# Linear attention and a Hadamard feed-forward on one core: the running state in split fp32r, and the joints of the feed-forward in another order

## The chip, the cores and the metric

The kernel runs on one core of a Trainium2 chip. The metric is device time in microseconds (us) of one execution, less being better. The core's engines work side by side, each through its own instructions in order: TensorE (PE in the profile, PEld for its weight loads), VectorE (DVE), ScalarE (ACT), GpSimd (POOL). SyncE (SP) issues all DMA transfers of this kernel.

## The reference

One layer of a transformer on 4096 tokens of 512 features: causal linear attention with 16 query heads and 4 key/value heads of 128, then a feed-forward whose inputs pass a Walsh-Hadamard transform; a layer norm follows each. Cut to what matters:

```python
q = rope(x @ Wq.T); k = rope(x @ Wk.T); v = x @ Wv.T      # 16, 4, 4 heads of 128
qf, kf = elu(q) + 1, elu(k) + 1
def step(carry, inp):
    state, z = carry
    q_s, k_s, v_s = inp
    state = state + k_s[..., :, None] * v_s[..., None, :]
    z = z + k_s
    return (state, z), (q_s @ state) / (q_s @ z + 1e-6)
out = scan(step, zeros, (qf, kf, v)) @ Wo.T
x = layernorm(x + out)
h = fwht(x * SU_ug) / 64
h = silu(h @ W_gate.T * sg) * (h @ W_up.T * su)
h = fwht(h * SU_dp) / 64
x = layernorm(x + h @ W_down.T * sd)
```

All is in fp32. The kernel keeps fp32 accuracy on fp32r matmuls by splitting an operand into a high half (rounded to fp32r, an ACT copy) and a low half (the difference, a DVE or POOL subtraction): a product of two such operands takes three matmuls, high x high, high x low and low x high (`hilo` is the helper, lines 95 and 96).

## The kernel before, in words

**Attention** (0 to about 935 us). Two passes `s` over the key/value heads (two of them, `g`, in each pass), each over 16 blocks of 256 tokens: 32 blocks `n`. A block's rows are cut into four chunks of 64 tokens. Within a chunk attention is done by scores: `scores` (lines 380 and 381) multiplies queries with the chunk's keys, `A` is masked by POOL (394). What lies before the chunk comes from the running state, a 128 x 128 matrix per head and chunk: `av` (414) adds q x state and A x v into `ps_num`, and `ps_den` (415) is the denominator.

The state of chunk c is the sum over all tokens before it, plus its first one, so the tiles are shifted by a token: `nat_k` transposes k from its second column on into `kfn`, and `vs` holds v shifted by one row. `state` (337) multiplies `kfn` with `vs` as plain fp32, four matmuls per block and head: rows 0 to 63 and rows 0 to 127 of each half block. DVE adds the state of before (`s32`), ACT and DVE split the result into `sh` and `sl` (353, 355). `vd` holds v's halves for the sums in `av`, each chunk's rows once in the order of the tile; the first row of a chunk is zero there (`rowm_s` is the row mask), since the state holds it already. `proj_v`, `proj_k` and `proj_q` are the projections (241, 288), `rope` rotates.

The main loop runs over 128 slots (n, g, p), two chunks each. A slot issues, in this order: the query projection five slots ahead (`QA`), parts of the next block's k and v and of the states, the scores one slot ahead (`SA`), and `av`. The generators are advanced by hand with `go`; the program is laid out by a scheduler with a simulated timeline, so instructions on one engine may pass each other where an operand is late in that timeline. `pin` keeps an instruction in its written place. In slots 4 to 51 and 62 to 109 `wcomb` sums feed-forward weights on POOL.

**Output projection** (to about 1326 us): 32 tiles of 128 tokens, `wo_tile` (173), `norm_o`, layer norm. Beside it `prep_down` transforms the down weights and `front` (two transposes and a Hadamard matmul per pair of tiles) prepares the feed-forward input for the first three quarters; each quarter is combined for Strassen's scheme with seven products, whose operands are `YKEY`, `WKEY` and the order `SEQ`.

**Up-projection** (to about 1980 us): 32 passes `n` = (quarter f, p), seven products of two matrices (1033). The last four fronts (`ff_front`, i from 12) run inside passes 1 to 6. The results go to `hop_d` in DRAM by `late_puts`, three at a time.

**Down-projection**: eight units (f, jp) of seven products (1187), the first two units interleaved; the operands come back from DRAM (`h_load`, `h_split`, for the first product `h_split_x`), the residual rows by `y_load`, and each product is added to them by `acc` (1197) on DVE. PSUM has eight banks; each stage's pools take them in the order of allocation, so a bank is free once the instruction that last used it in the stage before is done.

Of the kernel before, what the change touches and what calls it, by code (L numbers as in the profile page):

```python
# [20 lines left out]
NB = NTOK // TB  # L21
# [22 lines left out]
def kernel(  # L44
# [3 lines left out]
    cs, ident, had, sel, rowm, out,  # L48
# [30 lines left out]
    rowm_s = cpool.tile([128, 1], F32, name="rowm_s")  # L79
# [8 lines left out]
    def load_raw(src):  # L88
        pool, tag = first.pop(0) if first else (praw, "raw")
        raw = pool.tile([128, 512], F32, tag=tag, name="raw")  # L90
        dma(raw, src)
        return raw
# [86 lines left out]
    with ExitStack() as es:  # L179
# [14 lines left out]
        G.memset(neg1, -1.0)  # L194
        W = {}
# [36 lines left out]
        def proj_v(n):  # L232
# [11 lines left out]
            v32 = pe.tile([128, 2, 256], F32, tag="v32", name="v32")  # L244
            S.activation(v32, ps, AF.Copy)
            vhl = p1.tile([128, 2, 2, 256], F32R, tag="vhl", name="vhl")
            S.activation(vhl[:, 0], ps, AF.Copy, scale=rowm_s)
            yield
            V.scalar_tensor_tensor(vhl[:, 1], ps, rowm_s, vhl[:, 0].bitcast(F32), ALU.mult, ALU.subtract)
            vd = p2.tile([128, 2, 4, 256], F32R, tag="vd", name="vd")  # L250
            for half in range(2):
                for par in range(2):
                    dst = vd[half * 64:half * 64 + 64].rearrange("p l (t r) d -> p l t r d", r=2)[:, :, :, par]
                    dma(dst, vhl[par * 64:par * 64 + 64])
            vs = p1.tile([128, 2, 256], F32, tag="vs", name="vs")
            dma(vs[63:128], v32[0:65])
            dma(vs[0:63, 1], v32[65:128, 0])
            if b:
                dma(vs[0:63, 0], blk[n - 1]["v32"][65:128, 1])
            else:  # L260
                G.memset(vs[0:63, 0], 0.0)
            B.update(v32=v32, vd=vd, vs=vs)

        def rope(ps, csb, f, stay=False):
# [8 lines left out]
            x1 = ps if stay else pe.tile([128, 2, 256], F32, tag="x1", name="x1", bufs=3)  # L273
# [45 lines left out]
        def nat_k(n):  # L319
# [6 lines left out]
            kfn = p1.tile([128, 2, 2, 128], F32, tag="kfn", name="kfn")  # L326
            S.activation(kfn, pt, AF.Copy)
            B["kfn"] = kfn
            B["S"] = []

        def state(n, g):
# [3 lines left out]
            for i in range(4):  # L335
                r = slice(0, 64 * (i % 2) + 64)
                T.matmul(ps[:, i], B["kfn"][r, g, i // 2], B["vs"][r, i // 2, g * 128:(g + 1) * 128],  # L337
                         start=True, stop=True)
# [16 lines left out]
            V.tensor_tensor(sl, s32, sh.bitcast(F32), ALU.subtract)  # L355
# [41 lines left out]
        def av(n, g, p):  # L397
# [19 lines left out]
            num = p3.tile([128, 4, 2, 64], F32, tag="num", name="num")  # L417
# [3 lines left out]
            if p == 1:  # L421
                ds = pout.tile([4, 256], F32, tag="ds", name="ds", bufs=2)
# [53 lines left out]
        first.extend([(praw, "raw")] * 3 + [(p3, t) for t in ("num", "s32", "sh", "sl") for _ in range(3)])  # L476
# [7 lines left out]
        dma(rowm_s, rowm)  # L484
# [27 lines left out]
        run(proj_v(0))  # L512
        weights_q(0, 0)
# [4 lines left out]
        nat_k(0)  # L518
# [15 lines left out]
        for i, (n, g, p) in enumerate(slots):  # L534
# [18 lines left out]
            if sl == (0, 0):  # L553
# [6 lines left out]
                gs2 = state(n, 1)  # L560
                go(gs2)
# [7 lines left out]
            elif sl == (1, 0):  # L569
                if nxt:  # L570
                    nat_k(n + 1)
            else:
                gs1 = state(n + 1, 0) if nxt else None
                go(gs1)
# [11 lines left out]
            elif sl == (0, 1):  # L586
                go(gv)
            elif sl == (1, 1):
                go(gs1)
            av(n, g, p)  # L590
# [112 lines left out]
    def front(i, y2, spool, ptr, phd, alloc):  # L703
        f, c = divmod(i, 4)
        d = alloc[1]([128, 2, 4, 128], F32, "fd")
        for e in range(2):
# [7 lines left out]
            yield  # L714
            ps = phd([128, 4, 128], "ps_hd")
# [68 lines left out]
    with ExitStack() as es:  # L784
        p2 = late["c2"] = es.enter_context(tc.tile_pool(name="c2", bufs=2, reuse_waits="tile"))
        pwo = es.enter_context(tc.tile_pool(name="pwo", bufs=3, space=PSUM, reuse_waits="tile"))
        pfd = es.enter_context(tc.tile_pool(name="pfd", bufs=1, space=PSUM, reuse_waits="tile"))
        pon = es.enter_context(tc.tile_pool(name="pon", bufs=2, space=PSUM, reuse_waits="tile"))

# [184 lines left out]

    def h_split_x(n, his, los):
        HOP[n, 0] = []
        for qd, raw in enumerate(HR.pop((n, 0))):
            hi, lo = (x[qd // 2][:, 2 * (qd % 2):2 * (qd % 2) + 2] for x in (his, los))
# [3 lines left out]
    with ExitStack() as es:  # L982
# [8 lines left out]
        def ff_front(i):  # L991
            y2 = []
            for e in range(2):
                y = utile("y_nat")
# [11 lines left out]
        for n in range(NS):  # L1006
# [11 lines left out]
            if n in (1, 2, 4, 5):  # L1018
                step(fr, 9)
                fr = ff_front(12 + (1, 2, 4, 5).index(n))  # L1020
            new = {}
            for s, tag in enumerate(SEQ):
# [41 lines left out]
                if p == 7:  # L1064
# [4 lines left out]
                    elif s == 0:  # L1069
                        hx = [xtile([128, 4, 256], F32R, "hxh") for _ in range(2)]  # L1070
                        hx += [ytile([128, 4, 256], F32R, x) for x in ("hxl", "hxl", "hxh", "hxh", "hxl", "hxl")]
                        h_split_x(0, hx[0:2], hx[2:4])
                        h_load(1, 0)
                    elif s == 2:
                        split_b(0)
                        load_b(1)
                    elif s == 3:
                        h_split_x(1, hx[4:6], hx[6:8])
# [25 lines left out]
    with ExitStack() as es:  # L1104
# [6 lines left out]
        def y_load(n):  # L1111
            f, jp = units[n]
            YN[n] = []
            for half in range(2):
                y = (pd.tile([128, 2, 512], F32, tag="yn", name="yres") if half else
                     xtile([128, 2, 512], F32, "yres"))
                for j in range(2):
                    dma(y[:, j], y_d[8 * f + 2 * (2 * jp + j) + half])
                YN[n].append(y)

# [7 lines left out]
        def finish(n, half):  # L1128
            f, jp = units[n]
            y = YN[n][half]  # L1130
# [21 lines left out]
        y_load(0)  # L1152
        y_load(1)
        for idx, (n, s) in enumerate(order):
# [8 lines left out]
            if idx > 0:  # L1163
                for put in late_puts[:3]:
                    put()
# [103 lines left out]
```

## Time and profile before

| | before |
|---|---|
| median of 3 runs | 2309.88 us (2309.2 to 2312.54) |
| the profiled execution | 2307.71 us |
| its span in the profile | 2306.0 us |
| granted TensorE clock, mean | 0.994 |
| PE, DVE, ACT, POOL busy | 2260.5, 1765.5, 1394.5, 1281.7 us |
| DMA queue | 481.45 MB, 68.0% of 16 engines |

A row of the profile names a line of the kernel, the engine, the operation, the tiles (result<-operands), the shape and the count; then its busy time, the mean of one in ns, and the time for which the engine was idle before such instructions, with what ended it. Matmuls are pipelined, so their durations overlap: two that start 0.11 us apart can show 0.28 us each. In the chain of waits each instruction has the time from the one before it.

### The profile page before, as it was taken

To read this page: it belongs to the slowest core of one execution; us is meant where nothing else is said; L and a number is where in the kernel's file an instruction comes from. 1 tells how busy PE (TensorE), PEld (TensorE's weight loads), DVE (VectorE), ACT (ScalarE), POOL (GpSimd) and SP (SyncE) were. 2 spreads that over 40 slices of the span, in tenths; PEclk is the share of its full clock that TensorE was granted. 3 is DMA by queue.
4 is the path that set the end of the run, shared out by engine and by line. 5 is a ranking of instruction groups with operands and counts; after the bars stand their busy time and mean duration, and the time that the engine had idled before them with its cause. 6 is when DMAs were issued, how large, how long until landed. Compare 5 with 4: busy or idle time off the path is not lost.

```text
span 2306.0 us, 42216 instructions
## 1 busy us (share of the span) xinstructions
PE 2260.5 (98%) x14432; PEld 2005.5 (87%) x14432; DVE 1765.5 (77%) x2684; ACT 1394.5 (60%) x2515; POOL 1281.7 (56%) x1063
## 2 busy tenths in 40 slices
PE   8999999999999999899999999999999999899998
PEld 7999999899999998688878878788788888899998
DVE  8888888888888878688898766776766766675555
ACT  7777777777777767344443566655555655464553
POOL 5556666555555546468787435665555555633332
PEclk9999999999999999999999999999999999999999
DMA  6665665555655554889988976876766757887673
GB/s 195 176 180 171 181 185 173 165 157 150 168 168 150 161 152 130 309 268 270 291 282 262 294 240 212 249 244 192 227 209 187 224 186 212 265 274 242 227 253 119
DMA packets 369527, 484.15 MB, mean 210 GB/s; under 512 B 68670, under 2 KB 224384, under 8 KB 365344
## 3 DMA queue, kind: packets, MB, share of 16 engines
q1 hardware_dynamic: 369312, 481.45, 68.0%
q8 instruction: 114, 1.87, 0.3%
q14 instruction: 101, 0.83, 0.1%
HBM read 282.76 MB, written 156.76 MB: 191 GB/s over the span
## 4 chain that ended last, share of the span: by engine, by line
PE 88%; DMA 5%; DVE 3%; POOL 2%; ACT 1%; issue 1%; SPq 0%; POOLq 0%; DVEq 0%; ACTq 0%
PE ps_qk L288 17%; PE ps_a L1033 14%; PE ps_wo L173 13%; PE ps_da L1187 7%; PE ps_b L1033 7%; PE ps_num L414 6%; PE ps_v L241 4%; PE ps_s L337 4%; PE ps_c L1033 4%; PE ps_db L1187 4%; PE ps_dc L1187 2%; PE ps_sc L380 1%; PE ps_sc L381 1%; PE ps_den L415 1%; DMA rb<-rec_d 1%
## 5 line engine op out<-in xcount | busy, mean ns | idle before, releaser
L288 PE MATMUL ps_qk<-xh,wh 128*128 128x256 f32 x1280 | 355.6, 278 | 0.0
L288 PE MATMUL ps_qk<-xl,wh 128*128 128x256 f32 x1280 | 355.3, 278 | 0.0
L288 PE MATMUL ps_qk<-xh,wl 128*128 128x256 f32 x1280 | 354.7, 277 | 0.0
L394 POOL TENSOR_SCALAR_AFFINE_SELECT A<-A 64x512 fp32r<-64x512 f32 x256 | 212.1, 829 | 241.0 <-DVE am L390 144.2
L96 DVE TENSOR_TENSOR wol<-A,woh 128x512 fp32r<-128x512 f32 x217 | 229.0, 1060 | 108.8 <-ACT woh L95 95.5
L1015 POOL TENSOR_TENSOR cc<-cc 128x512 f32<-128x512 f32 x96 | 149.9, 1562 | 285.8 <-ACT cc L1012 162.4
L270 POOL TENSOR_TENSOR sw<-sw,csb 128x512 f32<-128x512 f32 x160 | 208.0, 1300 | 135.3 <-ACT sw L269 121.3
L288 PEld LDWEIGHTS ps_qk<-xh,wh 128*128 128x128 f32 x1280 | 241.0, 188 | 3.1
L288 PEld LDWEIGHTS ps_qk<-xh,wl 128*128 128x128 f32 x1280 | 240.8, 188 | 0.9
L288 PEld LDWEIGHTS ps_qk<-xl,wh 128*128 128x128 f32 x1280 | 240.9, 188 | 0.3
L95 ACT ACTIVATE woh<-A 128x512 fp32r<-128x512 f32 x217 | 135.6, 630 | 131.3 <-PE ps_b L1033 76.7
L95 ACT ACTIVATE hah<-hraw 128x512 fp32r<-128x512 f32 x216 | 133.2, 629 | 120.1 <-PE ps_da L1187 55.5
L96 POOL TENSOR_TENSOR hal<-hraw,hah 128x512 fp32r<-128x512 f32 x78 | 105.8, 1360 | 179.3 <-PE ps_da L1187 64.1
L1033 PE MATMUL ps_a<-yoh,woh 128*128 128x512 f32 x512 | 202.2, 396 | 2.6 <-DVE yp L901 2.3
L1033 PE MATMUL ps_a<-yol,woh 128*128 128x512 f32 x512 | 202.5, 395 | 0.0
L1033 PE MATMUL ps_a<-yoh,wol 128*128 128x512 f32 x512 | 199.6, 395 | 0.0
L96 DVE TENSOR_TENSOR hal<-hraw,hah 128x512 fp32r<-128x512 f32 x138 | 110.5, 811 | 90.9 <-PE ps_da L1187 34.0
L173 PE MATMUL ps_wo<-wh,oh 128*128 128x512 f32 x372 | 148.5, 399 | 3.1 <-ACT oh L95 3.1
L1040 ACT ACTIVATE sv<-ps_a,wsc 128x512 f32<-128x512 f32 x192 | 127.2, 680 | 39.3 <-PE ps_a L1033 39.2
L173 PE MATMUL ps_wo<-wh,ol 128*128 128x512 f32 x372 | 147.8, 397 | 0.0
L173 PE MATMUL ps_wo<-wl,oh 128*128 128x512 f32 x372 | 147.8, 397 | 0.0
L271 DVE TENSOR_TENSOR ps_qk<-ps_qk,csb 128x512 f32<-128x512 f32 x160 | 111.2, 695 | 33.0 <-ACT sw L269 31.9
(280 smaller groups left out, 7359.5 us busy)
## 6 DMA issues: line engine op xcount, KB each, us to landing
hraw<-hop_d SPq DMA_DIRECT2D x224, 256.0 KB
vd<-vhl SPq DMA_DIRECT2D x128, 256.0 KB
num_d<-num SPq DMA_DIRECT2D x128, 256.0 KB
rb<-rec_d SPq DMA_DIRECT2D x128, 256.0 KB
hop_d<-hS SPq DMA_DIRECT2D x128, 256.0 KB
nt<-num_d SPq DMA_DIRECT2D x31, 1024.0 KB
A<-in_wug_dram SPq DMA_DIRECT2D x93, 256.0 KB
hop_d<-cc SPq DMA_DIRECT2D x64, 256.0 KB
```

The lines of the kernel that those rows point to most:

```text
L95: i = S.activation(hi, src, AF.Copy)
L96: j = eng.tensor_tensor(lo, src, hi.bitcast(F32), ALU.subtract)
L173: T.matmul(ps, l[:, h], r, start=i == 0, stop=i == 47)
L270: G.tensor_tensor(sw, sw, sinb, ALU.mult)
L271: V.tensor_tensor(ps, ps, cosb, ALU.mult)
L288: T.matmul(ps[:, j], W[key][wa][:, k * 128:(k + 1) * 128], B[xa][:, k], start=i == 0, stop=i == 11)
L394: G.affine_select(ah, ah.bitcast(F32), pattern=[[0, 8], [1, 64]], compare_op=ALU.is_ge, fill=0.0, base=0, channel_multiplier=-1)
L414: T.matmul(ps[:, c2], l, r, start=i == 0, stop=i == len(ops) - 1)
L1015: G.tensor_tensor(x, x, c.pop(("g", q)), ALU.mult)
L1033: T.matmul(ps, w[:, u, k], y[:, k], start=first and i == 0, stop=i == 5, skip_group_check=not first)
L1040: S.activation(x, ps, AF.Copy, scale=sc)
L1187: T.matmul(ps[:, j], ops[qd][al][:, r, js], BW[s][bl][ip], start=first and i == 0, stop=i >= 45 or last and i == 23, skip_group_check=True)
```

## The change

Five things are changed.

1. The running state is made from split halves. `kfn` holds a high and a low half of k, `vst` a high and a low half of shifted v, each twice (index `u`): once with rows 64 to 127 zero (for the boundary in the middle of a half block), once whole. So both states of a half block come from one matmul of 256 columns, three of them for the three products. The fp32 copy `v32` and the tile `vs` are gone.
2. `vst`, `vcar` and the two tiles `VD` last for the whole stage; their zero rows are written once at the start by DVE and ACT, so the row mask `rowm` is gone, and the transfers leave those rows out. `vcar` carries the tail of v from block to block.
3. The low half of every second state (`sl`, g = 1) is subtracted by POOL in place of DVE. The low half of k is a new subtraction on DVE.
4. Buffers: `num` has two in place of three, `ds` one for two, `x1` two for three.
5. Joints: the PSUM pool `pwo` is allocated after `pfd` and `pon`; the last four fronts start in passes 1, 3, 5, 8 in place of 1, 2, 4, 5, take their rows into raw buffers, and wait one step more before their Hadamard matmul; the first h halves go to raw and weight buffers; `y_load` is made for half a unit at a time, for the first two units within the last up pass; the sum of product (2, 0) is put off by one product; the last block's second state is made a slot earlier.

```diff
@@ setup of attention
+        vst = pe.tile([128, 2, 2, 2, 256], F32R, name="vst", bufs=1)
+        vcar = pe.tile([128, 2, 256], F32R, name="vcar", bufs=1)
+        VD = [p2.tile([128, 2, 4, 256], F32R, tag="vd", name="vd") for _ in range(2)]
+        def zero(eng, dst):
+            src = ones4[0:dst.shape[0], 0:1, None].to_broadcast(list(dst.shape))
+            if eng is S:
+                S.activation(dst, src, AF.Copy, scale=0.0)
+            else:
+                V.tensor_scalar(dst, src, 0.0, None, ALU.mult)
+        for l in range(2):
+            for k in range(2):
+                zero(S if k else V, VD[k][:, l])
+                zero(S if k else V, vst[64:128, l, k, 0:1])
+            zero(S, vst[0:64, l, 0])
@@ proj_v
-            v32 = pe.tile([128, 2, 256], F32, tag="v32", name="v32")
-            S.activation(v32, ps, AF.Copy)
-            S.activation(vhl[:, 0], ps, AF.Copy, scale=rowm_s)
+            S.activation(vhl[:, 0], ps, AF.Copy)
             yield
-            V.scalar_tensor_tensor(vhl[:, 1], ps, rowm_s, vhl[:, 0].bitcast(F32), ALU.mult, ALU.subtract)
+            V.tensor_tensor(vhl[:, 1], ps, vhl[:, 0].bitcast(F32), ALU.subtract)
+            vd = VD[n % 2]
             for half in range(2):
                 for par in range(2):
-                    dma(dst, vhl[par * 64:par * 64 + 64])
+                    dst = vd[half * 64 + 1:half * 64 + 64].rearrange("p l (t r) d -> p l t r d", r=2)[:, :, :, par]
+                    dma(dst, vhl[par * 64 + 1:par * 64 + 64])
-            dma(vs[63:128], v32[0:65])
-            dma(vs[0:63, 1], v32[65:128, 0])
-            if b:
-                dma(vs[0:63, 0], blk[n - 1]["v32"][65:128, 1])
+            dma(vst[63:128, :, :, 1], vhl[0:65])
+            dma(vst[63:64, :, :, 0], vhl[0:1])
+            for u in range(2):
+                dma(vst[0:63, :, 1, u], vhl[65:128, :, 0])
+                if b:
+                    dma(vst[0:63, :, 0, u], vcar[0:63])
...
+        def carry(n):
+            if n < N and n % NB < NB - 1:
+                dma(vcar[0:63], blk[n]["vhl"][65:128, :, 1])
@@ nat_k
-            S.activation(kfn, pt, AF.Copy)
+            kfn = pe.tile([128, 2, 2, 2, 128], F32R, tag="kfn", name="kfn", bufs=1)
+            S.activation(kfn[:, 0], pt, AF.Copy)
...
+            yield
+            V.tensor_tensor(kfn[:, 1], pt, kfn[:, 0].bitcast(F32), ALU.subtract)
@@ state
-            for i in range(4):
-                r = slice(0, 64 * (i % 2) + 64)
-                T.matmul(ps[:, i], B["kfn"][r, g, i // 2], B["vs"][r, i // 2, g * 128:(g + 1) * 128],
-                         start=True, stop=True)
+            for j in range(2):
+                for i, (k, v) in enumerate(((0, 0), (0, 1), (1, 0))):
+                    T.matmul(ps[:, 2 * j:2 * j + 2], B["kfn"][:, k, g, j], vst[:, v, j, :, g * 128:(g + 1) * 128],
+                             start=i == 0, stop=i == 2)
...
-            V.tensor_tensor(sl, s32, sh.bitcast(F32), ALU.subtract)
+            (G if g else V).tensor_tensor(sl, s32, sh.bitcast(F32), ALU.subtract)
@@ main loop: nat_k is a generator, its second part a few instructions later
             elif sl == (1, 0):
                 if nxt:
-                    nat_k(n + 1)
+                    gn = nat_k(n + 1)
+                    go(gn)
+                    carry(n + 1)
@@ front
             hilo(hl[:, 0], hl[:, 1], ps)
             yield
+            if i >= 12:
+                yield
@@ output projection
-        pwo = es.enter_context(tc.tile_pool(name="pwo", bufs=3, space=PSUM, reuse_waits="tile"))
...

+        pwo = es.enter_context(tc.tile_pool(name="pwo", bufs=3, space=PSUM, reuse_waits="tile"))
@@ up-projection
-            if n in (1, 2, 4, 5):
-                step(fr, 9)
-                fr = ff_front(12 + (1, 2, 4, 5).index(n))
+            if n in (1, 3, 5, 8):
+                step(fr, 12)
+                fr = ff_front(12 + (1, 3, 5, 8).index(n))
...
                     elif s == 0:
-                        hx = [xtile([128, 4, 256], F32R, "hxh") for _ in range(2)]
+                        hx = [praw.tile([128, 2, 256], F32R, tag="raw", name="hxh") for _ in range(3)]
+                        hx.append(wres.tile([128, 2, 256], F32R, tag="w", name="hxh"))
...
                         h_load(1, 0)
+                        y_load(0, 0)
+                        y_load(1, 0)
@@ down-projection
-        y_load(0)
-        y_load(1)
...
+            if s == 1 and n < 2:
+                y_load(n, 1, pd)
...
+            if todo:
+                acc(*todo)
+                todo = None
+            if s == 0 and n == 2:
+                todo = (y0, lo, ps)
```

## The prediction

> **What bounds the kernel now.** I read the engine totals first, then the table by stretches of time, then the chain of waits inside one block of attention, then PE's gaps one by one. Engine totals (busy us, share of the span, instructions):
>
> ```profile
> PE 2260.5 (98%) x14432; PEld 2005.5 (87%) x14432; DVE 1765.5 (77%) x2684; ACT 1394.5 (60%) x2515; POOL 1281.7 (56%) x1063
> ```
>
> PE is idle for 45.5 us in all, so whatever removes PE time is worth its full length as long as no other engine becomes the bound. The stretches (length, then busy us of PE, PEld, DVE, ACT, POOL, clock, DMA share, GB/s) show where another engine is near:
>
> ```profile
> 130.00:230.00 100.00, 100.00 (x819) 95.20 (x819) 89.50 (x141) 74.77 (x140) 59.60 (x58) 1.00 0.57 164
> 530.00:630.00 100.00, 100.00 (x816) 94.79 (x814) 85.99 (x137) 71.88 (x133) 53.36 (x57) 1.00 0.56 155
> 930.00:1030.00 100.00, 92.76 (x408) 73.37 (x407) 74.42 (x120) 43.67 (x87) 55.21 (x41) 0.98 0.88 295
> 1930.00:2030.00 100.00, 93.58 (x614) 85.77 (x613) 63.89 (x70) 51.71 (x91) 61.84 (x43) 0.97 0.82 250
> ```
>
> In attention (0 to 930 us) PE is full, but DVE stands at 86 to 90%. The two other rows are the joints between stages, where PE loses 7.2 and 6.4 us. The chain of waits in attention (start, length, what) lies wholly on PE; one stretch of it:
>
> ```profile
> 569.77 2.72 PE ps_qk L288 x24
> 572.50 1.67 PE ps_s L337 x8
> 574.16 0.36 PE ps_num L414 x3
> ```
>
> and the rows of the running state and of a projection, by form:
>
> ```profile
> L288 PE MATMUL ps_qk<-xh,wh 128*128 128x256 f32 x1280 | 355.6, 278 | 0.0
> L337 PE MATMUL ps_s<-vs,kfn 128*128 128x128 f32 x256 | 62.3, 325 | 0.0
> L337 PE MATMUL ps_s<-vs,kfn 64*128 64x128 f32 x256 | 62.1, 322 | 1.1 <-ACT kfn L327 0.6 <-DVE s L348 0.5
> ```
>
> The means overlap, since matmuls are pipelined; prices come from the chain. A state has four fp32 matmuls of 128 columns, recorded as eight (512 records for 32 blocks x 2 groups x 4), and takes 1.67 us: 0.209 us a record. The 24 projection matmuls (fp32r, 256 columns) take 2.72 us: 0.113 each.
>
> **The change part by part.**
>
> *Running state on PE.* A block of 256 tokens takes 28.02 us on the chain (projection of v to projection of v, 560.97 to 588.99). Two states take 3.34 of it; its other 212 records share 24.68 us, 0.116 each. After, a state is six fp32r matmuls of 256 columns (three products for each of two token halves): 6 x 0.116 = 0.70 us. Saved: 2 x (1.67 - 0.70) = 1.94 us a block, over 32 blocks 62.2 us. The Trainium skill speaks against this: "FP8 and Floating Point Precision", section "TensorE Precision Notes", counts a true fp32 matmul as four passes; with the 55.6 ns between 128-column matmuls that "TensorE: Matmul & The Clock Gate" gives (section "Wait — 56ns, not 53.3ns?"), a state is an estimated 4 x 4 x 0.056 = 0.89 us and the whole change would be worth only 64 x (0.89 - 0.70) = 12 us. The trace has 1.67 us for the same thing, and the row decides: 62 us.
>
> *DVE.* Added per block: the low half of k, a subtraction read from PSUM; nearest row `ql<-ps_qk`, 685 ns, so 32 x 0.685 = +21.9 us. The low half of v loses its row mask: 746 to about 685 ns, -2.0. Half of the `sl` subtractions go to POOL: 32 x 0.891 = -28.5. Sum -8.6 us. *POOL* gains 32 subtractions with two SBUF inputs; its own rows for that shape run 1.36 us (`hal`) to 1.68 (`xl`); at 1.45 it is +46 us, from 56 to about 66% of a shorter stage. What that does to DVE I can only bound: DVE's `ql<-sw,qh` (two SBUF inputs) averages 979 ns, `ql<-ps_qk,qh` 685. The skill ("SBUF — State Buffer", "Who interferes with whom") says that a DVE instruction with two SBUF inputs contends with a POOL instruction that reads SBUF and that the loser blocks fully: as a worst case the whole 46 us would come back on DVE. By the row, about 0.3 us is lost per such instruction with POOL 60% busy; 8 points more POOL give some 0.04 us on six instructions, 0.2 us a block, +6 us. I take the row. DVE's total in attention thus stays at about 803 - 9 + 6 = 800 us, while PE's need falls to 930 - 62 = 868: 92%. In the first half of attention, where x is also split, it is worse: the block at 203 to 231 us shows 25.19 us of DVE, which becomes about 25.1 of 26.1, 96%.
>
> *ACT* loses the fp32 copy of v (597 ns x 32 = 19 us) and the masked scale (682 to 597 ns, 3 us): 72% before, no limit.
>
> *SP and the copies of v.* Before: three `vs` transfers and four `vd` a block. After: `vd` stays at four; `vst` takes one of 65 rows, one of a single row, two of 63 rows, two more from the carry tile where a block precedes, and the carry tile itself one: seven in place of three. SP's rows price an issue:
>
> ```profile
> 564.68 1.63 SPq L58 DMA_DIRECT2D vs<-v  x2
> 566.40 3.40 SPq L58 DMA_DIRECT2D vd<-vhl  x4
> ```
>
> 0.82 to 0.85 us each, so 7 x 0.84 - 2.47 = +3.4 us a block. Adding up SP's rows for the block 561 to 589 gives 18 us; it becomes 21.6 of 26.1. Behind those seven stand the stores of `num` and `ds`, the x loads two blocks ahead, the wcomb loads and stores. `num` (three buffers to two), `ds` (two to one) and `x1` (three to two) are reused 13, 13 and some 13 us later, and ACT waited only 1.9 us in all for a `num` store: priced at nothing while SP's lag stays below a slot of 6.5 us; at most 1 us a block, 30 us, if it does not. The bytes added, about 0.65 MB a block, raise a DMA share of 0.57 by some 0.08: cover enough. One-tile `vhl` and `kfn` were one-tile before.
>
> *Friction in attention.* With DVE at 92 to 96% and SP at 83%, PE will not stay gapless. Bounds: 3 us (as gapless as now) and 58 us (DVE keeps all the idle time it has now, see the rival). In the densest stretch that the trace has, DVE is 90% busy and PE shows no gap, so I am nearer the low end: 0.7 us a block in the first half, 0.25 in the second, +15 us.
>
> *Start.* Zeroing the lasting tiles costs ACT about 4 us and DVE 3; ACT is free from 2.1 to 3.4 us, DVE to 4.1 us, so +1.5 (0 to 3).
>
> *Joints*, from PE's gaps in the timeline (start, length, what, gap before it and its releaser), and DVE's row that explains the largest:
>
> ```profile
> 1328.49 0.50 PE L1033 MATMUL ps_a<-yoh,woh 128*128 128x512 f32 x1 [2.26 <-DVE yp L901]
> 1376.21 0.50 PE L716 MATMUL ps_hd<-fhl,hadr 128*128 128x512 f32 x1 [1.34 <-ACT fhl L95]
> 1383.51 0.66 PE L709 MATMUL ps_tr<-idt,y_nat 128*128 128x128 f32 x4 [0.95 <-DMA y_nat<-y_d]
> 1986.43 0.58 PE L1187 MATMUL ps_dc<-wdh,hal 128*128 128x256 f32 x1 [5.21 <-DVE hal L96]
> 2072.86 0.38 PE L1187 MATMUL ps_da<-wdh,hah 128*128 128x256 f32 x1 [1.16 <-DVE yres L1197]
> 1984.19 0.69 DVE L1197 TENSOR_TENSOR yres<-ps_da,yres 128x512 f32<-128x512 f32 x1 [5.14 <-DMA yres<-y_d]
> ```
>
> The PSUM pools of the output projection swap places, so that the first feed-forward banks were last used by `pfd`, not by the last `ps_wo`: 2.26 us. The fronts inside the up-projection get one more step before their Hadamard matmul and start further apart, with y in the raw buffers: 1.34 + 0.95. At the start of the down-projection DVE stood behind a sum whose `yres` rows were asked for only at 1978.9 us; the loads for both first units move to the last up-projection pass, ahead of the h loads: up to 5.21, and the smaller wait of 1.21 before it. The deferred sum of (2, 0) takes away 1.16. Together 12.1 us. The loads moved go past the `hop_d` stores and h loads on SP, so what is late next may be an h tile (POOL waited up to 4.5 us for `hraw`), and the h halves of the two first units now sit in raw and weight buffers, which must be free: I count 9, with 3 and 13 as ends. The 3.10 us at 945.83 (output projection behind `rec_d` loads) is not touched in its cause; nothing.
>
> **Sum.** -62.2 + 15 + 1.5 - 9 = -54.7 us against the profiled execution (2307.71 us; span 2306.0). That gives 2253.0; the median of the runs, 2309.88, lies 2.2 above that execution, so 2255 us. About 0.2% (5 us) is what a measurement of this kernel can tell from no change.
>
> **The rivals.**
> *DVE becomes the bound.* If DVE keeps the idle time that it has (2.8 us of the 28 at 203 to 231, 4.2 at 561 to 589, most of it short waits for ACT's `sw` and `qh`), a block takes 25.1 + 2.8 = 27.9 in the first half and 23.7 + 4.2 = 27.9 in the second, and attention gains 0.1 x 32 = 4 us; halfway between this and gapless is a gain of 33. Against the extreme: those waits are for results of PE work, which now comes sooner. With half: -33 + 1.5 - 9 = -40, 2269; the extreme is 2298. Chance of a result nearer to this than to the forecast: 0.2.
>
> *The copies of v land too late (slower).* After the change the state needs `vst`, which is filled from the split v, behind four `vd` issues on the same queue. v's low half is ready near 565.7 in the block shown; eight issues at 0.84 us end at 572.4. The chain's DMA pieces run from issue to use 4.1 us (`raw<-in_x_t`) to 4.9 (`rb<-rec_d`), so the last copy lands at about 576.9, while PE comes to the state at 572.5: 4.4 us of stall in 31 blocks, +136 against -70 of the other terms, 2375 us. It decides from 2.2 us of stall a block. Against it: the state is first read at 583.5 (`ps_num<-qh,sh` after the next group's scores), so 8 us of slack lie behind it, and the order of instructions is laid out by a simulated timeline that already slips projections between scores and sums where an operand is late; if it puts the state a few matmuls later, nothing waits. Chance 0.1, with 2315 to 2375 as its range.
>
> *The six new matmuls are not cheaper.* If a state matmul keeps 0.209 us whatever its type, six take 1.25 us and the gain is 64 x 0.42 = 27 us; less 8 of friction: -27 + 8 + 1.5 - 9 = -26, 2283. Against it: every fp32r row of 256 columns runs at 0.113 to 0.127. Chance 0.04.
>
> **How the numbers follow.** Forecast 0.66 (2238 to 2268), DVE bound 0.2 (2262 to 2298), price kept 0.04, late copies 0.1. Faster: 0.66 + 0.2 + 0.04 less a little for the extreme ends, 0.88; slower 0.1; same 0.02. The range takes in friction at 3 and joints at 13 with the start at nothing (2309.9 - 62.2 + 3 - 13 = 2238) and, above, most of the DVE case: 2238 to 2288. What is left out is the late copies and the DVE extreme, under 2 in 10.
>
> **What the changed profile would show.** Right: `ps_s` as 384 records of 128x256, 0.70 us for six on the chain; blocks 26 to 27 us apart; DVE at 91 to 95% in attention, POOL at 65%; no gap above 2 us near the start of the down-projection. DVE bound: PE below 97% busy in the first half, its gaps released by DVE (`A`, `sl`, `ql`). Late copies: gaps before `ps_s` released by DMA `vst`. Wrong altogether: a span above 2300 with PE gapless, that is, new PE time that I do not see in the diff.

## The result, and the profile after

| | before | after |
|---|---|---|
| median of the runs | 2309.54 us (2308.2 to 2312.54) | 2439.75 us (2438.14 to 2441.04) |
| ratio, with 95% interval | 1 | 1.0561 (1.0545 to 1.0577) |
| span of the profiled execution | 2306.0 us | 2439.3 us |
| granted TensorE clock, mean | 0.994 | 0.961 |
| first matmul of the output projection (`ps_wo`) | 945.8 us | 1085.3 us |

The changed kernel is 130 us slower, where 55 us less was forecast. All of it lies in attention: the first `ps_wo` comes 139.5 us later, and what follows is 6.1 us shorter than before. It is the rival of the late copies, which had a chance of 0.1, and it is 65 us dearer than priced there.

The page of the kernel after: engine totals, the granted clock in 40 slices (tenths of full speed), and the group of the running state:

```profile
PE 2279.3 (93%) x14304; PEld 2054.8 (84%) x14304; DVE 1750.5 (72%) x2690; ACT 1380.9 (57%) x2489; POOL 1310.5 (54%) x1093
...
PEclk9989999999999989899999999999999999999999
...
L358 PE MATMUL ps_s<-vst,kfn 128*128 128x256 f32 x384 | 79.4, 337 | 117.4 <-DMA vst<-vhl 106.6
```

PE is idle for 160 us where it was for 45.5, and its busy time has not gone down by the 62 us that the cheaper state should save: it went up by 19. The second number says that something else slowed the matmuls. Busy time hides that, so the stretches by clock come next (columns as before: length, then busy us of PE, PEld, DVE, ACT, POOL, clock, DMA share, GB/s), at the times shown of before (at 930 us the kernel after is still in attention):

```profile
130.00:230.00 100.00, 89.73 (x691) 87.67 (x691) 76.55 (x120) 63.77 (x119) 55.71 (x54) 0.91 0.55 171
530.00:630.00 100.00, 87.56 (x677) 85.63 (x676) 70.54 (x117) 59.65 (x109) 46.41 (x49) 0.91 0.48 147
930.00:1030.00 100.00, 87.76 (x685) 86.18 (x685) 73.59 (x120) 60.54 (x113) 48.53 (x51) 0.91 0.49 145
1930.00:2030.00 100.00, 100.00 (x430) 80.53 (x429) 69.98 (x78) 57.30 (x93) 54.81 (x36) 1.00 0.69 215
```

In attention two things are wrong at once: PE is idle for 10 to 12% of the time, and the granted clock is 0.91 on the mean where it was 1.00. DVE, ACT, POOL and the DMA engines are all less busy than before, so none of them is the bound. The waits of PE (total us, times, longest) name what it waits for:

```profile
PE ps_s L358 <- DMA vst<-vhl: 106.6, 39, 4.8
PE ps_w L172 <- ACT qh L94: 7.3, 1, 7.3
PE ps_v L256 <- ACT wh L94: 7.2, 1, 7.2
PE ps_dc L1226 <- DVE hal L95: 5.4, 1, 5.4
```

One block shows how the wait comes about. First SP's queue in the timeline (start, length, what):

```profile
614.68 4.20 SPq L58 DMA_DIRECT2D vd<-vhl  x4
618.98 3.73 SPq L58 DMA_DIRECT2D vst<-vhl  x4
622.82 1.74 SPq L58 DMA_DIRECT2D den_d<-ds  x2
```

then PE's timeline in the same block:

```profile
621.73 0.28 PE L307 MATMUL ps_qk<-xh,wh 128*128 128x256 f32 x1
626.17 0.98 PE L358 MATMUL ps_s<-vst,kfn 128*128 128x256 f32 x3 [4.16 <-DMA vst<-vhl]
626.94 0.41 PE L307 MATMUL ps_qk<-xl,wh 128*128 128x256 f32 x1
627.16 0.41 PE L307 MATMUL ps_qk<-xh,wl 128*128 128x256 f32 x1
...
629.81 0.28 PE L435 MATMUL ps_num<-qh,sh 128*128 128x256 f32 x1
629.92 0.28 PE L435 MATMUL ps_num<-ql,sh 128*128 128x256 f32 x1
```

v's low half is ready at 614.66. SP issues the four `vd` transfers first, at 1.05 us each, then the four `vst` transfers, until 622.71; the state starts 3.46 us after that. PE reached it at 622.01 and stood for 4.16 us. The rows behind show the second cost: matmuls of 256 columns start 0.22 us apart at 626.94, and 0.12 us apart again from 629.2 on. The records of the clock show it as well. The wait fills the stretch of the first row here, and in the next 3.41 us the granted clock is 0.50 (columns as above):

```profile
622.26:625.67 3.41, 0.00 (x0) 0.00 (x0) 1.22 (x2) 0.41 (x1) 1.80 (x2) 1.00 0.59 146
625.67:629.09 3.42, 2.92 (x14) 2.95 (x15) 0.00 (x0) 0.00 (x0) 0.00 (x0) 0.50 0.78 238
629.09:632.50 3.41, 3.41 (x30) 3.34 (x30) 3.02 (x6) 2.50 (x5) 0.94 (x2) 1.00 0.90 245
```

The old kernel had written the same order (`vd`, then the shifted copies), but its copies read `v32`, the fp32 copy that ACT finished 1.6 us before the split halves, and the scheduler had pulled them ahead; that is why its SP rows show `vs` before `vd`. The change made both sets of transfers read `vhl`. They now become ready together, and the written order stands.

What does the new state cost where nothing is late? This one, 20 us earlier in the trace after, is not held up:

```profile
602.51 0.88 PE L358 MATMUL ps_s<-vst,kfn 128*128 128x256 f32 x6
603.23 0.28 PE L401 MATMUL ps_sc<-qh,khl 128*128 128x256 f32 x1
```

0.72 us for six matmuls, against 1.67 before. The saving that the change was priced at is there.

### The profile page after: what moved, and what is told of

It is laid out like the page before. It is cut to its first block, busy times and chain, and to the rows that moved or that the text cites. A ratio compares the mean times of both kernels' runs of the same rounds, so it can differ in the third digit from the quotient of the medians.

```text
span 2439.3 us, 42199 instructions
## 1 busy us (share of the span) xinstructions
PE 2279.3 (93%) x14304; PEld 2054.8 (84%) x14304; DVE 1750.5 (72%) x2690; ACT 1380.9 (57%) x2489; POOL 1310.5 (54%) x1093
## 5 line engine op out<-in xcount | busy, mean ns | idle before, releaser
L307 PE MATMUL ps_qk<-xh,wh 128*128 128x256 f32 x1280 | 374.1, 292 | 0.0
L307 PE MATMUL ps_qk<-xh,wl 128*128 128x256 f32 x1280 | 373.6, 292 | 0.0
L307 PE MATMUL ps_qk<-xl,wh 128*128 128x256 f32 x1280 | 373.4, 292 | 0.0
L415 POOL TENSOR_SCALAR_AFFINE_SELECT A<-A 64x512 fp32r<-64x512 f32 x256 | 199.1, 778 | 250.6 <-DVE am L411 194.1
L307 PEld LDWEIGHTS ps_qk<-xh,wh 128*128 128x128 f32 x1280 | 256.1, 200 | 2.7
L307 PEld LDWEIGHTS ps_qk<-xl,wh 128*128 128x128 f32 x1280 | 256.8, 201 | 1.0
L307 PEld LDWEIGHTS ps_qk<-xh,wl 128*128 128x128 f32 x1280 | 256.1, 200 | 0.8
L358 PE MATMUL ps_s<-vst,kfn 128*128 128x256 f32 x384 | 79.4, 337 | 117.4 <-DMA vst<-vhl 106.6
L358 PEld LDWEIGHTS ps_s<-vst,kfn 128*128 128x128 f32 x384 | 64.4, 231 | 126.0 <-issue 98.7
L369 DVE TENSOR_TENSOR s<-ps_s,s 128x256 f32<-128x256 f32 x124 | 51.7, 417 | 140.1 <-PE ps_s L358 139.5
```

Of the source, the lines that this page charges most:

```text
L307: T.matmul(ps[:, j], W[key][wa][:, k * 128:(k + 1) * 128], B[xa][:, k], start=i == 0, stop=i == 11)
L358: T.matmul(ps[:, 2 * j:2 * j + 2], B["kfn"][:, k, g, j], vst[:, v, j, :, g * 128:(g + 1) * 128], start=i == 0, stop=i == 2)
L369: V.tensor_tensor(s32[:, i:i + 2], ps[:, i:i + 2], prev.to_broadcast([128, 2, 128]), ALU.add)
L415: G.affine_select(ah, ah.bitcast(F32), pattern=[[0, 8], [1, 64]], compare_op=ALU.is_ge, fill=0.0, base=0, channel_multiplier=-1)
```

## The experiments

Theory after the first look: the place of `vst` in SP's queue makes PE wait, and the half clock after each wait makes it dearer. Rivals: the number of transfers (seven or more for three) or the load on DVE makes the kernel slow whatever the order; or the clock falls for another reason and the waits follow from it.

**e1: the `vst` transfers ahead of the `vd` transfers.** The only edit is that the lines of `vst` stand above the `vd` loop in `proj_v`.

```diff
+            dma(vst[63:128, :, :, 1], vhl[0:65])
+            dma(vst[63:64, :, :, 0], vhl[0:1])
...
             for half in range(2):
                 for par in range(2):
                     dma(dst, vhl[par * 64 + 1:par * 64 + 64])
-            dma(vst[63:128, :, :, 1], vhl[0:65])
-            dma(vst[63:64, :, :, 0], vhl[0:1])
...
```

Expected:

> The changed kernel with one edit: in proj_v the vst transfers are issued ahead of the four vd transfers. Theory A (the state waits because its copies stand behind vd on the SP queue, 4 x 1.05 us, and the idle stretch lets the TensorE clock drop): the wait for vst shrinks from 4.1 us a block to under 1, the clock returns to 0.99, 2240 to 2275 us. Theory B (the copies land late by themselves, small rows and a long way from issue to landing, wherever they stand): a gap of 2 to 3 us a block stays, over 2330 us. Theory C (DVE or SP is the bound once the state is cheap): no wait for vst, but PE gaps released by DVE, 2275 to 2310 us.

Measured: 2322.8 us, ratio 1.0049 (1.0033 to 1.0064), clock 0.983. No wait for `vst` is left, and 117 us are back. But it is still slower than before. The waits of ACT in e1 name a new one:

```profile
ACT num L439 <- DMA num_d<-num: 64.8, 19, 6.3
```

and an instance of it, SP first, then ACT, both from the timeline:

```profile
596.75 3.33 SPq L58 DMA_DIRECT2D vst<-vhl  x4
600.13 4.97 SPq L58 DMA_DIRECT2D vd<-vhl  x4
605.20 0.66 SPq L58 DMA_DIRECT2D num_d<-num  x1
```

```profile
611.42 0.60 ACT L439 ACTIVATE num<-ps_num 128x512 f32<-128x512 f32 x1 [4.42 <-DMA num_d<-num]
```

Eight transfers in a row hold SP for 8.4 us, the store of `num` stands behind them, and with two `num` buffers in place of three ACT stops for 4.42 us; `sh` and `A` are then late for PE, which waits 8.3 us for `sh` and 17.5 us for `A` in e1. Whether a third `num` buffer alone would have taken ACT's wait away was not tried. So e1 separates the two parts of SP's trouble: `vst` behind `vd` stops PE at once, and eight transfers in one burst stop ACT.

**e9: the old kernel with its copies kept behind `vd`.** The opposite of e1, made on the kernel before: fp32 state, three `vs` transfers, old joints. The last argument of `dma` keeps a transfer in its written place.

```diff
-                    dma(dst, vhl[par * 64:par * 64 + 64])
+                    dma(dst, vhl[par * 64:par * 64 + 64], True)
-            dma(vs[63:128], v32[0:65])
-            dma(vs[0:63, 1], v32[65:128, 0])
+            dma(vs[63:128], v32[0:65], True)
+            dma(vs[0:63, 1], v32[65:128, 0], True)
```

Expected:

> The kernel before (fp32 state, three vs and four vd transfers, old joints) with one thing changed: the two vs transfers of a block are kept behind its four vd transfers on SP's queue. In the kernel before they stand ahead, because the fp32 copy of v is ready 1.6 us before the split halves. Theory (the place in the queue is what costs, not the number of transfers and not the new matmuls): in the block at 561 to 589 us of before, vd would be issued from 566.4 to 569.8, vs to 571.4, and land 3.5 us later (the time that the kernel after shows from the last vst issue to the state's start), at 574.9; the state stands at 572.5, or some 0.7 us later where projections pass it: 1.7 to 2.4 us of wait for DMA vs a block, 50 to 75 us in all, and some matmuls at half clock on top. 2360 to 2400. Rival (the seven transfers or the DVE load made the kernel after slow): no wait above 0.5 us a block, 2310 to 2320.

Measured: 2371.55 us, ratio 1.0246 (1.0203 to 1.0290), clock 0.980. The state's group by form, and one block of PE's timeline:

```profile
L337 PE MATMUL ps_s<-vs,kfn 64*128 64x128 f32 x256 | 65.1, 336 | 41.4 <-DMA vs<-v 20.2 <-ACT qh L366 11.3 <-issue 5.3
```

```profile
583.38 2.07 PE L337 MATMUL ps_s<-vs,kfn 64*128 64x128 f32 x8 [1.58 <-DMA vs<-v]
585.10 0.56 PE L288 MATMUL ps_qk<-xl,wh 128*128 128x256 f32 x1
585.46 0.41 PE L380 MATMUL ps_sc<-qh,khl 128*128 128x256 f32 x1
585.67 0.41 PE L381 MATMUL ps_sc<-ql,khl 128*64 128x256 f32 x1
```

The order alone costs the old kernel 63 us. Counted from the starts of PE's records, the waits before the first matmul of a state add up to 46 us (1.4 in before), 1.5 a block and a little under the 1.7 to 2.4 expected. Matmuls at half clock add some 24 us (how this is counted stands in the section on the prediction). The rival that blamed the number of transfers or DVE falls: neither was changed here. The state does not read `qh`, which the row also names; a wait for several semaphores is put down to one of them, and how much of those 11.3 us is the copy of v is not told by the row.

**e2: the state made later.** The state of head group 0 is moved from the block before to the first slot of its own block, some 34 matmuls later on PE; SP's order stays as in the kernel after.

```diff
-                gs1 = state(n + 1, 0) if nxt else None
-                go(gs1)
+                gs1 = None
...
+                if n:
+                    gs1 = state(n, 0)
+                    go(gs1)
+                    go(gs1)
+                    go(gs1)
```

Expected:

> The changed kernel with the transfers as they are, but the state of head group 0 moved from the last slot of the block before into the first slot of its own block: some 34 matmuls (about 4 us) later on PE, still ahead of its first reader. Theory A: a wait of 4.1 us is covered by 4 us of other matmuls, 2245 to 2290 us. Theory B gives the same here if its lateness is the same 4 us; a queue that falls further behind with every block (SP saturated) would give 2350 us or more. If the early place of the state is needed (its readers wait for sh and sl instead), PE gaps of about 3 us before ps_num, over 2350 us.

Measured: 2375.22 us, ratio 1.0282 (1.0259 to 1.0306), clock 0.975. From PE's waits:

```profile
PE ps_s L358 <- DMA vst<-vhl: 55.0, 39, 3.5
```

The wait is halved, not gone: as many times, half as long. This is what the prediction's argument of slack amounts to when it is tried: moving the state back by some 34 matmuls, 4 us at 0.12 each, takes half of the wait away. The rest is lost because the copies come later too: in the block at 577 to 593 us v's low half is ready 4.8 us after the projection of v on PE, where the block shown of the kernel after has 2.7. Why DVE makes it later was not traced.

**e3: other work in front of the state.** 32 matmuls whose result is overwritten by the state, put ahead of the state of head group 0 in each block; they add work and change nothing in what the kernel computes (`FILL` is 32).

```diff
+            if g == 0 and n:
+                for i in range(FILL):
+                    T.matmul(ps[:, 0:2], W["q", s, 0, i % 4][0][:, 0:128], B["xh"][:, i % 4], start=True, stop=True)
```

Expected:

> The changed kernel with 32 extra fp32r matmuls of 256 columns per block ahead of the state of head group 0, written to its PSUM bank and overwritten by it: 3.7 us of PE work that should lie inside the wait. It measures the clock by itself. If the drop of the granted clock after each idle stretch is a cost of its own (about 160 us more at half clock than before, so some 75 us of work lost): 2350 to 2385 us, mean clock 0.98 or more. If the waits alone are the cost: 2430 to 2450 us, with the idle time turned into busy time.

Measured: 2488.39 us, ratio 1.0766 (1.0746 to 1.0786), clock 0.974. PE's wait for `vst` fell to 56.9 us, but in 55 places where it was 39. The layout moved the state as well: these matmuls begin 76 behind v's projection in nearly every block, where the state of the kernel after stands 78 to 98 behind it. It was to show the clock by itself and does not: waits and clock went down together. Inconclusive.

**e5: `vst` first, and `vd` a slot later.** e1's order, and the `vd` transfers taken out of `proj_v` and issued for the next block after the low half of its k.

```diff
+        def put_vd(n):
+            vd, vhl = blk[n]["vd"], blk[n]["vhl"]
+            for half in range(2):
+                for par in range(2):
...
+                    dma(dst, vhl[par * 64 + 1:par * 64 + 64])
...
                     go(gn)
                     carry(n + 1)
+                    put_vd(n + 1)
```

Expected:

> e1 (vst first) with the four vd transfers not behind vst at once, but after the low half of k, a slot later; they are first read a slot and more after that. In e1 no wait for vst is left, but ACT waited 64.8 us in all for num_d stores before it could write num (two buffers) again, because those stores stood behind vst and vd on the SP queue; DVE, PE and the clock then followed. Theory D (the queue of SP, through num, is what is left of the loss): ACT's wait for num_d falls to under 20 us, 2240 to 2285 us. Theory C (DVE is the bound): no change beyond 10 us, 2310 to 2325.

Measured: 2274.65 us, ratio 0.9849 (0.9831 to 0.9866), clock 0.991: 165 us less than the kernel after, 35 less than before. A stretch of attention in e5:

```profile
530.00:630.00 100.00, 100.00 (x851) 99.00 (x850) 91.19 (x147) 74.92 (x137) 59.34 (x62) 1.00 0.65 194
```

PE is gapless at full clock with all the transfers of the change still there and DVE at 91%. In its timeline SP issues the two sets apart, with the `num` and `den` stores between them:

```profile
580.97 3.38 SPq L58 DMA_DIRECT2D vst<-vhl  x4
584.45 0.44 SPq L58 DMA_DIRECT2D num_d<-num  x1
584.99 0.58 SPq L58 DMA_DIRECT2D den_d<-ds  x2
585.62 0.81 SPq L58 DMA_DIRECT2D vcar<-vhl  x1
586.48 4.38 SPq L58 DMA_DIRECT2D vd<-vhl  x4
```

Same bytes, same count, another order: this settles the main cause.

**e6: `vd` spread over two later slots.** As e5, but two of the four transfers at the end of each of the block's last two slots.

```diff
+            if g and nxt:
+                put_vd(n + 1, p)
```

Expected:

> As e5, with two of the vd transfers at the end of the third slot and two at the end of the fourth, so that a num store never stands behind more than two of them. Theory D: at or below e5, 2235 to 2280 us, faster than both kernels. Theory C: 2310 to 2325.

Measured: 2306.58 us, ratio 0.9985 (0.9976 to 0.9993). Now `vd` itself is late, for the sums of the next block. PE's waits:

```profile
PE ps_num L437 <- DMA vd<-vhl: 16.0, 12, 3.0
```

Of the three places tried for `vd`, the first holds up `vst` and `num` (e1 and the kernel after), the last holds up `av` (e6), and the one between them does neither (e5).

**e7: e1 with the `num` stores issued by ACT.** This takes the stores off SP instead of moving `vd`.

```diff
-            dma(num_d[2 * b + p][:, gg], num.rearrange("p h c q -> p (h c q)"))
+            nc.scalar.dma_start(num_d[2 * b + p][:, gg], num.rearrange("p h c q -> p (h c q)"))
```

Expected:

> e1 with the num stores issued by ACT in place of SP, so that they never stand behind vst and vd; the price is 128 issues on ACT, about 0.35 us each if they cost there what they cost on SP. Theory D: ACT's wait for num_d goes, 2250 to 2295 us. Theory C: 2310 to 2335.

Measured: 2329.6 us, ratio 1.0088 (1.0072 to 1.0105), no better than e1. ACT's waits:

```profile
ACT ds L444 <- DMA den_d<-ds: 37.6, 15, 4.1
```

The wait for `num` is down from 64.8 to 3.6 us, and the next store in the line takes its place: `ds` has one buffer, and its stores still stand behind the burst.

**e8: e5 with both `sl` subtractions on DVE,** as in the kernel before.

```diff
-            (G if g else V).tensor_tensor(sl, s32, sh.bitcast(F32), ALU.subtract)
+            V.tensor_tensor(sl, s32, sh.bitcast(F32), ALU.subtract)
```

Expected:

> e5 with both low halves of the state (sl) on DVE as in the kernel before, so 28 us more of DVE and 40 us less of POOL. If DVE is near its bound in attention: 10 to 30 us slower than e5. If DVE has slack and POOL's order was what delayed the masks: equal or up to 10 us faster.

Measured: 2290.14 us, ratio 0.9914 (0.9892 to 0.9936), 15.5 us more than e5. PE's largest wait in attention is now for a DVE result (`PE ps_sc L404 <- DVE A L415: 12.2, 14, 2.1`; 5.8 us in 4 places in e5). Moving `sl` to POOL, which takes 24.6 us off DVE in e5 (32 x 769 ns), is worth 15 us of time once PE is no longer held up by SP: DVE is that near to being the bound.

**e4: the joints alone,** in the kernel before, attention untouched; the edit is part 5 of the change without the last block's state (front, output projection, up- and down-projection).

```diff
-            if n in (1, 2, 4, 5):
+            if n in (1, 3, 5, 8):
...
```

Expected:

> The kernel before with the joints alone changed (PSUM pools, fronts, y loads, first h halves, put-off sum), attention untouched. From the stages of the two profiles: output projection 4.5 us shorter, up-projection 3.1 shorter, down-projection 1.4 longer: 2303 us (2299 to 2307). The forecast had 2300 to 2301 for this part. If the joints cost time: over 2310.

Measured: 2301.03 us, ratio 0.9956 (0.9940 to 0.9972), 9.0 us less than the runs of before beside it, as forecast. But only some of it comes from the places forecast. PE's waits in e4:

```profile
PE ps_dc L1196 <- DVE hal L96: 5.2, 1, 5.2
...
PE ps_da L1196 <- DVE yres L1206: 2.6, 2, 1.7
PE ps_wo L173 <- ACT oh L95: 2.1, 1, 2.1
```

The 5.2 us at the start of the down-projection are all still there. What went: the 2.26 us between output and up-projection, 1.34 and 0.95 at the fronts, 1.21 before `ps_dc`, and 1.0 of the 3.10 before `ps_wo`, for which nothing was forecast. The wait that the put-off sum was to take away did not go either: 1.68 us in e4, 1.16 in before. In the profiles the up-projection is 4.1 us shorter, the stage before it 2.7, the down-projection 1.3 longer.

**e10, e11, e12: 32 bytes.** In e5 the gapless block of the second half takes 26.4 us, not the 26.1 of the forecast. The projection matmuls (`ps_qk`, 3840 of them) follow each other at 118.2 ns on the mean in e5 and in the kernel after, 114.0 in the kernel before, in e4 (114.0) and even in e9 (114.1); in e5 and in before it is the same in every 100 us of attention. The change took out `rowm_s`, a tile of one column, and in the layout of SBUF the weights `wh`, `wl` start 32 bytes lower against multiples of 64 (before: 32 above one, like `xh` and `xl`; after: on one, while `xh` and `xl` stayed 32 above). e10 puts an unused tile of 32 bytes back ahead of the weights in e5; e11 puts one into the kernel before, so that the same mismatch arises there; e12 moves `xh` and `xl` in the kernel before instead.

```diff
+    pad = cpool.tile([128, 8], F32, name="pad")
+    nc.gpsimd.memset(pad, 0.0)
     idt = cpool.tile([128, 128], F32, name="idt")
```

Expected of e10, e11, e12:

> As e5 (vd after the state), plus one unused tile of 32 bytes a partition ahead of the weights. Why: in every kernel with the new attention the projection matmuls (ps_qk) follow each other at 118.2 ns, in before at 114.0, at all times and under any load; the change took the tile rowm_s away, so that the weights wh and wl start 32 bytes lower than in before, while xh and xl keep their place within 64 bytes. Theory (the address of the weights against that of x sets the spacing): ps_qk goes back to 114 ns, 3840 x 4.2 ns = 16 us less than e5: 2259. Rival (the spacing comes from the heavier traffic of the new attention): ps_qk stays at 118 ns, 2275.

> The kernel before with the same unused tile of 32 bytes ahead of the weights, so that wh and wl lie 32 bytes off their place within 64 bytes, as they do in the kernel after; nothing else is changed. Theory (addresses): ps_qk goes from 114 to 118 ns, +16 us, 2326. Rival (traffic): no change, 2310.

> The kernel before with an unused tile of 32 bytes that moves xh and xl by 32 bytes and leaves the weights where they are. If what counts is whether the weights and x lie alike within 64 bytes, ps_qk goes to 118 ns, 2326. If what counts is the weights' own place, it stays at 114 ns, 2310.

Measured: e10 2270.42 us, 0.9824 (0.9810 to 0.9838); e11 2319.63, 1.0043 (1.0030 to 1.0055); e12 2320.51, 1.0049 (1.0035 to 1.0063). The same stretch in e11, then in e12:

```profile
530.00:630.00 100.00, 100.00 (x803) 95.23 (x802) 85.85 (x138) 70.95 (x131) 53.27 (x55) 1.00 0.49 143
```

```profile
530.00:630.00 100.00, 100.00 (x803) 95.23 (x802) 85.77 (x138) 70.88 (x131) 53.19 (x55) 1.00 0.50 141
```

803 matmuls in 100 us of gapless PE at full clock, where before has 816. An unused tile of 32 bytes on either side makes the old kernel 10 to 11 us slower; `ps_qk` stands at 117.8 ns in both. So what counts there for `ps_qk` is whether weights and x lie alike within 64 bytes, not where the weights lie. The operands of `ps_num` and `ps_sc` bear this out: in e11 both sides of each moved by the same 32 bytes, and their spacing stayed (118.7 and 116.9 ns in before, 118.9 and 116.9 in e11). But the rule is not complete. `ps_v` reads the same weights and x with the roles exchanged; it goes from 117.6 to 119.8 ns in e11 and e12, yet in e5 and in the kernel after, with the same mismatch, it stands at 117. The traffic theory falls for the kernel before. In e10 the spacing went back only to 115.4 ns, the block to 26.1 us, and the time fell by 4 us of the 16 expected (the intervals of e5 and e10 overlap): direction right, size not, and what holds the other 1.4 ns was not tried. e10 has the lowest median, 39 us below before.

## Why the prediction was wrong, point by point

**The state on PE: right.** Six matmuls take 0.72 us where 0.70 was forecast; a gapless block takes 26.4 us in e5 and 26.1 in e10 against 28.05 before and 26.08 forecast. So 1.65 to 1.9 us a block where nothing is late, 53 to 61 of the 62 us. Weighing the trace above the Trainium skill's four passes ("FP8 and Floating Point Precision", section "TensorE Precision Notes"), which made it 12 us, was right.

**The copies of v: the step that failed.** Its arithmetic was right. From v's low half to the state it counted 11.2 us (eight issues of 0.84, 4.5 to land); the block shown has 11.5 (8.05 and 3.46). It foresaw 4.4 us of wait in 31 blocks; the records show 4.16 in the block shown, and gaps before `ps_s` of 131 us in all, 114 of them before the first matmul of a state. What failed is the argument that reduced it to a chance of 0.1, that "8 us of slack lie behind it" and that the layout "already slips projections between scores and sums where an operand is late". The slack is that of the state's readers. PE takes its matmuls in the order laid out, so a late operand stops all that stands behind it: in the block shown projections and scores that read nothing of this state come only behind it, from 626.94 on. And the layout slipped the state by too little: in that block 84 matmuls stand between v's projection and the state, where e1 and e5 have 76, and PE reaches it 10.1 us after the end of the projection (611.9 to 622.0), against 8.6 before (563.9 to 572.5). Two printed lines would have shown it: `vs` stood ahead of `vd` in before only because it read another tile, and the diff takes that tile away.

**The clock: the term that was missing.** The rival's 2375 had no term for the clock; nor had it one for the spacing of `ps_qk` (16 us, in the sum below). Where matmuls follow each other 0.04 to 0.16 us later than usual, the surplus adds up to 71.5 us in attention after (752 matmuls), 29.6 before (313): 42 us more. By the records of the granted clock, 63 us of it lie in stretches at half clock after and 5 before. So half clock costs some 58 us, and other small delays are 17 us fewer than before. In e9 it is 29 us against 5, the 24 given there.

The Trainium skill has the mechanism ("TensorE: Matmul & The Clock Gate", section "Part 1: The HAM clock gate"): half clock after an idle window of some 3.4 us. The trace agrees for the wait of 4.16 us, but shorter ones suffice here: after the 1.58 us in e9 matmuls start 0.21 us apart as well. The stretches of e9 around that wait:

```profile
581.07:584.49 3.42, 1.84 (x13) 1.41 (x11) 1.90 (x3) 1.58 (x3) 3.06 (x3) 1.00 1.06 257
584.49:587.90 3.41, 3.41 (x17) 3.16 (x16) 2.17 (x5) 1.11 (x2) 0.00 (x0) 0.50 0.84 208
```

Within each trace looked at, all changes of the clock lie on one grid of 3.41 us. In the nine kernels with the new state, from 100 us on to 30 us before the end of attention, the clock fell to half after each of the 106 stretches of this grid in which PE had stood for 1.97 us or more, and after none of the 1978 with less than 1.84 (gaps of over 0.3 us between matmuls, counted from 0.12 us behind a start). In e9, with the fp32 state, the limit lies between 1.2 and 1.4 us. So the clock follows the waits, and not the other way round. The measurement decides: a part of a stretch is enough, and waits of 1.5 us a block are to be priced with the clock.

**Sum of attention.** Gaps between matmuls of over 0.16 us: 154 us after, 24 before, +130. Surplus of 0.04 to 0.16 us: +42, from half clock (+58) and other small delays (-17). The state: -62 by the count of matmuls at their usual distances. Start: +2.4 (1.5 forecast, up to 3). Distances within 0.04 us of the usual: +27, of which the shift of `ps_qk` is 16 (3840 x 4.2 ns); the other 11 were not traced. Together +139, as the trace has it.

**"Priced at nothing" for `num` and `ds`: wrong.** The condition was that SP's lag stays below a slot of 6.5 us; eight transfers in a row are 8.4 us. It is hidden in the kernel after, where PE waits first, and comes out in e1 as 64.8 us of ACT's waits. Its bound of 30 us was too low as well: e1 is 48 us above e5, its half clock included.

**DVE: right.** 800 us were forecast for DVE in attention; e5 has 799 (4 to 916 us). `kfn`'s low half takes 683 ns (685), POOL's `sl` 1.33 us (1.45). DVE was not the bound, but e8 shows it to be within 15 us of being so.

**Friction.** +15 was forecast. In e5, by the distances between blocks, 12 blocks of the first pass gain 15.4 us (1.3 each), 13 of the second 21.3 (1.6 each), the last two 5.1; the four around the pass change lose 5.7, the start 2.4, and the joint to the output projection gives back 4.0 (there is a new wait of 7.0 us for `qh`): attention ends 29.7 us earlier, against the 46 of the forecast.

**Joints: the size right, half of the parts wrong.** See e4. The `yres` rows were asked for earlier, and the wait for DVE's `hal` at the start of the down-projection did not move: the loads were not what that wait hung on, or something else now ends as late. It was not tried further.

## What to carry to other kernels

In these kernels transfers left SP's queue in the order in which their sources were ready, then in the written order. A change that makes two sets of transfers read the same tile can swap them without a line being moved, and the urgent set then has to be written first. Slack behind a result did not protect PE, which runs in order: ask where the instruction stands, not who reads its result. Price a wait of PE with the clock after it, and look at start addresses when a tile is added or removed ahead of matmul operands.

## What the runs showed of the hardware that was not expected

- Transfers between SBUF tiles are dear to issue: `vd` 0.70 us with 64 rows before, 0.81 with 63 rows after (medians of the issues), 1.05 each on the mean in the block shown, against 0.34 for a `num` store to DRAM.
- The granted clock changes on a grid of 3.41 us and falls to half when PE has stood for more than some 1.9 us of one stretch of it (nine kernels with the new state; 1.2 to 1.4 in e9). Matmuls then start 0.21 us apart in place of 0.12. In e9 all 11 waits of 1.5 us or more before a state were followed by this, and none of the 20 of up to 1.22 us. The mean granted clock over the stretches of 100 us in attention is then 0.91 after and 0.96 to 0.97 in e9.
- In the kernel before, weights and x that lie 32 bytes apart within 64 bytes cost 3.8 ns a projection matmul: 117.8 for 114.0 ns between `ps_qk` in e11 and e12, 10 to 11 us of 2309. For `ps_v` this held in e11 and e12 and not in e5.
